# Gated experts with residual: gate loads first, coefficients on GpSimd, operands around the openings made in another way and at other steps

## The chip, the cores and the metric

The kernel runs on one core of a Trainium2 chip. Five engines work side by side, each through its own instructions in order: TensorE (PE in the profile, with its weight loads as PEld), VectorE (DVE), ScalarE (ACT), GpSimd (POOL) and SyncE (SP), which here only issues DMA transfers. ACT issues two transfers as well. The metric is the device time of one execution in microseconds, as the median of several runs. The profile is of one further execution.

## The reference, cut to what matters

For each of 8 batch items `x[b]` (512 rows of 256) there are 8 experts and one shared expert, all of the same form, a gated product with an inner width of 1024:

```python
g = jnp.einsum('bsd,edf->ebsf', h, Wg)
u = jnp.einsum('bsd,edf->ebsf', h, Wu)
expert_outs = jnp.einsum('ebsf,efd->ebsd', jax.nn.silu(g) * u, Wd)
expert_output = jnp.einsum('be,ebsd->bsd', gating_probs, expert_outs)
shared = jnp.einsum('bsf,fd->bsd', jax.nn.silu(h @ Sg) * (h @ Su), Sd)
sg = shared_gate_prob[:, :, None]
return (1.0 - sg) * expert_output + sg * shared     # x + this is the output
```

So each hidden block of expert `e` and item `b` is scaled by one number, `gates[b, e] * (1 - shared_gate[b])`, or `shared_gate[b]` for the shared expert. All data is float32.

## The kernel before, in words

**Units.** The 8 items are worked in two halves of 4. A half runs over 9 experts, an expert over 2 groups of 4 blocks of 128 inner columns. That makes 36 units; a unit is 4 weight blocks against 4 items, for gate (`m = 0`) and up (`m = 1`), followed by the down products. Unit 0 opens the first half and unit 18 the second (`u.opens`); units 17 and 35 close them (`u.closes`).

**Fewer products.** The 256 input columns are two halves of 128, so a plain product of block i and item j takes two matrix products. The kernel takes fewer: it forms weights `at[i] = CI[i] * a + A` with `CI = (0, 1, -1, 2)` from the two halves `a`, `A` of a weight block, and item operands in the same manner (`turn_x`), computes the diagonal i = j (steps P and Q), and for the six pairs of `PAIRS` a shared product (R1) of differences `U`, `V` and two further products (R) of sums `W`, `VB`. This needs sums of operands on POOL and ACT, and of partial results (`z`, `Q`) on DVE and POOL. The down products use sums `T` and `sd` in the same spirit, two parts of four items each, and accumulate over the units of a half in `acc`.

**Item operands.** At the start of a half, `turn_x` transposes each item on PE into PSUM banks `po0`, `po1`, which ACT (line 155) and DVE (157, 159) copy out. The differences `V` and sums `VB` of the items are the same for all units of a half: they are made once, stored to DRAM (`scratch`), and loaded again by later units (lines 201 and 220). In the second half, three of the six pairs are made ahead by `make_forms`, during unit 17, and stored by `store_made`: DVE subtracts (175), ACT scales if needed (177), DVE adds (178), POOL adds (179), SP stores (186).

**Order.** A string of letters sets the order in each unit: a `G` is one step of gate and up, a `D` one down product of the unit before. `nG` counts the G steps, 52 in a unit: 16 for the diagonal and 6 for each pair. PE and POOL follow the program's order throughout (`manual_schedule`), ACT does in unit 0 only. DVE, SP and, after unit 0, ACT are ordered by a planner, by priority in program order and by when it thinks an instruction can run; on the chip each queue is then strictly in that order.

**Weights.** `load_w` brings gate and up of one block (two transfers of 128 KB, lines 261 to 268). `make_at(u, i)` forms the scaled weight: for `CI = 1` and `-1` one POOL operation, for `CI = 2` in all units but unit 0 an ACT scaling (line 280) and a POOL add (281); in unit 0 two POOL adds (290, 291). Blocks 0 to 2 are prepared in the unit before, block 3 at the unit's start (line 562).

**Coefficients.** `make_coef` loads the gates, spread to all partitions, through ACT's queue (lines 102, 107), and DVE makes the 9 x 8 table `coef` (109 to 112). `finish` reads it for each hidden block on DVE (line 361). It is called after the first products (644).

**The start.** `touch_banks` warms PE and ACT, then items and the weights of unit 0 are loaded in turn (lines 634 to 636), item 0 is turned, the P products of block 0 run, and the weights are formed:

```python
    for m in range(2):
        P_step(units[0], 0, m)
    for i in range(NI):
        make_at(units[0], i)
    make_coef()
```

Of the kernel before, what the change touches and what calls it, by code (L numbers as in the profile page):

```python
# [9 lines left out]
F32 = mybir.dt.float32  # L10
AF = mybir.ActivationFunctionType
ALU = mybir.AluOpType
# [4 lines left out]
def kernel(  # L17
# [32 lines left out]
    B, S, D = x.shape  # L50
    E, _, F = Wg.shape
    P = 128
# [5 lines left out]
    CI = (0.0, 1.0, -1.0, 2.0)  # L58
# [7 lines left out]
    const = ctx.enter_context(tc.tile_pool(name="const", bufs=1))  # L66
# [24 lines left out]
    gp = nc.gpsimd  # L91
    ve = nc.vector
# [3 lines left out]

    coef = const.tile([P, NE, B], F32, name="coef")

    def make_coef():

        gt = const.tile([P, B, E], F32, name="gt")
        nc.scalar.dma_start(
            gt.rearrange("p b e -> p (b e)"),
            gates.rearrange("b e -> (b e)").partition_broadcast(P),
        )
        sgt = const.tile([P, B], F32, name="sgt")
        nc.scalar.dma_start(sgt, shared_gate.partition_broadcast(P))
        rest = const.tile([P, B], F32, name="rest")
        ve.tensor_scalar(rest, sgt, -1.0, 1.0, ALU.mult, ALU.add)
        for e in range(E):  # L110
            ve.tensor_mul(coef[:, e, :], gt[:, :, e], rest)
        ve.tensor_copy(coef[:, E, :], sgt)

    scratch = {}
    back = {}
# [52 lines left out]
    def make_forms(h, p):  # L168

        i, j = PAIRS[p]  # L170
        d = CI[i] - CI[j]
        v, b0, b1 = (
            zpool.tile([P, S], F32, tag="z", name=f"f{k}{h}_{p}") for k in range(3)
        )
        ve.tensor_sub(v, xhub[h, i][:, 0], xhub[h, j][:, 0])
        if d != 1.0:
            nc.scalar.mul(v, v, 1.0 / d)
        ve.tensor_add(b0, v, xhub[h, j][:, 1])
        gp.tensor_tensor(b1, v, xhub[h, i][:, 1], ALU.add)
        made.append((h, p, (v, b0, b1)))  # L180
# [48 lines left out]
    def touch_banks():  # L229

        banks = [
            pool.tile([P, S], F32, tag=tag, name=f"touch{tag}{k}")
            for pool, tag, n in ((ps_g, "g0", 3), (ps_g, "g1", 3), (ps_o, "po0", 1), (ps_o, "po1", 1))
            for k in range(n)
        ]
        zero = zpool.tile([P, 2 * S], mybir.dt.bfloat16, tag="z", name="zero")[:, :S]
        ve.memset(zero, 0.0)
        warm = const.tile([P, 1], F32, name="warm")
        nc.scalar.activation(warm, ident[:, 0:1], AF.Silu)
        for bank in banks:  # L240
            nc.tensor.matmul(bank, zero[:, 0:P], zero, start=True, stop=True)
# [4 lines left out]
    units = []  # L246
    for h in range(NH):
        for e in range(NE):
            for g in range(GRP):
                u = Unit()  # L250
# [20 lines left out]
    def scaled_sum(out_, s, a, b, sub):  # L271

        if s in (1.0, -1.0):
            if s == 1.0:
                gp.tensor_tensor(out_, a, b, ALU.subtract if sub else ALU.add)
            else:
                assert not sub
                gp.tensor_tensor(out_, b, a, ALU.subtract)
        else:
            nc.scalar.mul(out_, a, s)  # L280
            gp.tensor_tensor(out_, out_, b, ALU.subtract if sub else ALU.add)  # L281

    def make_at(u, i):
        raw = u.raw[i]
        if CI[i] == 0.0:
            u.at[i] = raw[:, :, 1]
            return
        t = atpool.tile([P, 2, P], F32, tag="at", name=f"at{u.name}_{i}")
        if u.n == 0 and CI[i] == 2.0:
            gp.tensor_tensor(t, raw[:, :, 0], raw[:, :, 1], ALU.add)  # L290
            gp.tensor_tensor(t, t, raw[:, :, 0], ALU.add)
            u.at[i] = t
            return
        scaled_sum(t, CI[i], raw[:, :, 0], raw[:, :, 1], False)
        u.at[i] = t
# [4 lines left out]
    def plain(u, p):  # L300
        return u.n == 0 and p in PLAIN
# [28 lines left out]
    def load_d(u, pairs):  # L330
        for I in pairs:
            t = dpool.tile([P, 2, D], F32, tag="wd", name=f"wd{u.name}_{I}")
            r0 = (NI * u.g + 2 * I) * P
            nc.sync.dma_start(
                t,
                weights(u.e)[2][r0 : r0 + 2 * P].rearrange("(c p) d -> p c d", p=P),
            )
            s = dpool.tile([P, 4, P], F32, tag="sd", name=f"sd{u.name}_{I}")
            a11, a21 = t[:, 0, 0:P], t[:, 0, P : 2 * P]
            a12, a22 = t[:, 1, 0:P], t[:, 1, P : 2 * P]  # L340
            gp.tensor_tensor(s[:, 0], a21, a22, ALU.add)
            gp.tensor_tensor(s[:, 1], s[:, 0], a11, ALU.subtract)
            gp.tensor_tensor(s[:, 2], a11, a21, ALU.subtract)
            gp.tensor_tensor(s[:, 3], a12, s[:, 1], ALU.subtract)
            u.wd[I] = {
                1: a11, 2: a12, 3: s[:, 3], 4: a22, 5: s[:, 0], 6: s[:, 1], 7: s[:, 2]
            }

    def new_bank(u, m, name):
        return ps_g.tile([P, S], F32, tag=f"g{m}", name=f"{name}{m}_{u.name}")  # L350
# [16 lines left out]
    def P_step(u, i, m):  # L367
        bank = new_bank(u, m, f"c{i}{i}")
        u.bank[i, i, m] = bank
        nc.tensor.matmul(  # L370
            bank, u.raw[i][:, m, 0], xhub[u.h, i][:, 0], start=True, stop=True
        )
        t = ppool.tile([P, S], F32, tag="p", name=f"P{i}{m}_{u.name}")
        nc.scalar.copy(t, bank)  # L374
        u.Ps[i, m] = t
        for p in range(ZBANK):
            a, b = PAIRS[p]
            if max(a, b) == i and not plain(u, p):
                new_z(u, p, m, i, bank if u.n or p else None)

    def new_z(u, p, m, i, bank=None):

        o = sum(PAIRS[p]) - i
        z = zpool.tile([P, S], F32, tag="z", name=f"z{i}{o}{m}_{u.name}")
        if bank is None:
            gp.tensor_tensor(z, u.Ps[i, m], u.Qs[o, m], ALU.add)  # L386
        else:
            ve.tensor_add(z, bank, u.Qs[o, m])
        u.z[i, o, m] = z
# [159 lines left out]
    def gate_up(u, nxt):  # L549
# [11 lines left out]
        if u.n:  # L561
            make_at(u, 3)
# [23 lines left out]
        for p in range(len(PAIRS)):  # L586
# [3 lines left out]
            if nxt is not None:  # L590
                if p >= 2:
                    load_w(nxt, p - 2)
                    if p < 5:
                        make_at(nxt, p - 2)
# [34 lines left out]
    by_hand.enter_context(  # L629
        tc.manual_schedule(engines=HAND | {mybir.EngineType.Activation})  # L630
    )
    touch_banks()
    loaded = []
    for i in range(NI):
# [4 lines left out]
        next(turning)  # L639
    for m in range(2):  # L640
        P_step(units[0], 0, m)
    for i in range(NI):
        make_at(units[0], i)
    make_coef()
    behind, acc = iter(()), {}
    for u in units:
        final = u.closes
        nxt = units[u.n + 1] if u.n + 1 < len(units) else None
        g = gate_up(u, nxt)
        nG = 0  # L650
        for what in ORDER if u.n else FIRST:
            if what == "G":
                if nG == 4 and u.n:
                    for _ in behind:
                        pass
                    pv = units[u.n - 1]
                    load_d(pv, (1,))
                    if pv.opens:
                        acc = {}
                    behind = down(pv, acc, pv.closes)  # L660
                    if pv.closes:
                        load_back(pv.h, *BACK[0])
                        since_close = 0
                if final and nxt is not None:
                    if nG == 18:
                        turning = turn_x(u.h + 1, iopool, "io")
                    if nG >= 18 and nG % 3 == 0:
                        next(turning, None)
                    if nG in (42, 45, 48):
                        make_forms(u.h + 1, nG // 3 - 14)  # L670
                    if nG in (45, 48, 51):
                        store_made()
                next(g)
                nG += 1
                if nxt is None and nG in (18, 24, 30, 36, 42):
                    next(behind, None)
            elif u.n == 0:
                for _ in range(2):
                    next(turning, None)
            else:  # L680
                since_close += 1
                if ends and since_close >= BACK_AT[0]:
                    BACK_AT.pop(0)
                    turn_back(*ends.pop(0))
                next(behind, None)
        for _ in g:
            pass
        if u.n == 0:
            by_hand.close()
            by_hand.enter_context(tc.manual_schedule(engines=HAND))  # L690
        for _ in turning:
            pass
# [52 lines left out]
```

## Time and profile before

| what | value |
|---|---|
| median of 3 runs | 2525.23 us (2524.54 to 2525.8) |
| profiled execution, device time | 2527.06 us |
| its span, first to last instruction | 2525.2 us |
| mean granted TensorE clock | 0.998 |
| DMA | 242.94 MB, mean 96 GB/s |
| DVE `h` L361, 576 instructions | 741 ns each |
| POOL add of 128x512 (`z` L386) | 1281 ns each |
| POOL add of 128x256 (`wb` L281) | 741 ns each |
| ACT scaling of 128x256 (`at` L280), 35 instructions | 409 ns each |
| DVE coefficient products (L111), 8 instructions of 128x8 | 158 ns each |

An engine's busy time is the sum of its instructions; its share is of the span. "Idle before" an instruction is put down to the event that ended it. A line such as L361 is a line of the kernel. The chain of waits goes back from the last instruction, at each step to what released it. The busy share is an average over stretches with different limits, so what matters here is where PE, which is busy in nearly all of the span, is not fed.

### The profile page before, as it was taken

How to read it: one execution, taken by the hardware profiler on the slowest of the kernel's cores; microseconds unless marked ns; L12 is line 12 of the kernel's file. 1: busy time of each engine (PE TensorE's matmuls, PEld its weight loads, DVE VectorE, ACT ScalarE, POOL GpSimd, SP SyncE). 2: the span in 40 equal slices, each digit the busy share in tenths (PEclk: the TensorE clock that was granted, in tenths of full speed). 3: DMA queues.
4: the chain of work that ended last, by engine and by line, in shares of the span. 5: the costliest groups of instructions: out<-in, count | busy, mean ns of one | idle time of the engine just before them, and what ended most of it. 6: DMA issues, size and time to landing. Idle time of an engine off the chain costs nothing.

```text
span 2525.2 us, 22097 instructions
## 1 busy us (share of the span) xinstructions
PE 2501.5 (99%) x5900; PEld 1108.5 (44%) x5900; DVE 1491.3 (59%) x2252; ACT 1143.7 (45%) x2081; POOL 1917.4 (76%) x2067
## 2 busy tenths in 40 slices
PE   8999999999999999999999999999999999999999
PEld 3444444444444444444444444444444444444444
DVE  6655555555555555555775555565565555555556
ACT  3344444444444444444333444444444444444443
POOL 5878777777777778777797777777777777777874
PEclk9999999999999999999999999999999999999999
DMA  3422322333333223332434322232233332332322
GB/s 130 135 82 88 96 88 88 96 97 99 96 88 100 88 83 92 88 92 90 156 126 125 92 86 89 87 95 90 84 100 96 100 95 89 99 89 80 88 87 79
DMA packets 181179, 242.94 MB, mean 96 GB/s; under 512 B 13888, under 2 KB 122432, under 8 KB 181056
## 3 DMA queue, kind: packets, MB, share of 16 engines
q1 hardware_dynamic: 180768, 241.49, 31.7%
q8 instruction: 49, 0.80, 0.1%
q14 instruction: 74, 0.61, 0.1%
q10 hardware_dynamic: 288, 0.04, 0.0%
HBM read 227.84 MB, written 13.63 MB: 96 GB/s over the span
## 4 chain that ended last, share of the span: by engine, by line
PE 96%; DVE 2%; DMA 1%; POOL 1%; issue 1%; ACT 0%; SPq 0%; ACTq 0%; DVEq 0%; POOLq 0%
PE po L488 33%; PE c L442 28%; PE c L429 14%; PE c L401 10%; PE c L370 10%; DVE h L361 0%; DMA sgt<-ondB_sharedgateprob_dram 0%; DMA w<-in_L_cond_Wu_dram 0%; DVE c L434 0%; POOL T L461 0%; POOL z L386 0%; DMA xin<-in_x_dram 0%; PE pto L133 0%; DVE c L433 0%; PE c L414 0%
## 5 line engine op out<-in xcount | busy, mean ns | idle before, releaser
L442 PE MATMUL c<-b,wb 128*128 128x512 f32 x1720 | 810.6, 592 | 1.0 <-DVE c L433 0.5
L386 POOL TENSOR_TENSOR z<-P,Q 128x512 f32<-128x512 f32 x430 | 538.8, 1281 | 114.9 <-DVE Q L407 72.5
L361 DVE SCALAR_TENSOR_TENSOR h<-sg,coef,c 128x512 f32<-128x512 f32 x576 | 426.2, 741 | 230.6 <-PE c L442 220.1
L503 ACT COPY acc<-po 128x512 f32<-128x512 f32 x477 | 279.0, 585 | 585.0 <-PE po L488 582.2
L355 ACT ACTIVATE sg<-c 128x512 f32<-128x512 f32 x576 | 342.1, 595 | 372.3 <-PE c L442 196.8
L442 PEld LDWEIGHTS c<-b,wb 128*128 128x128 f32 x1720 | 325.9, 190 | 409.6 <-issue 386.1
L461 POOL TENSOR_TENSOR T<-h,h 128x512 f32<-128x512 f32 x284 | 358.0, 1278 | 135.0 <-PE po L488 91.7
L488 PE MATMUL po<-T,sd 128*128 128x512 f32 x864 | 435.4, 593 | 4.8 <-ACT po L479 3.2
L429 PE MATMUL c<-v,u 128*128 128x512 f32 x860 | 433.7, 592 | 3.0 <-DVE h L361 2.0
L433 DVE TENSOR_TENSOR c<-z,c 128x512 f32<-128x512 f32 x286 | 198.6, 694 | 330.9 <-ACT sg L355 253.5
L461 POOL TENSOR_TENSOR T<-h,T 128x512 f32<-128x512 f32 x284 | 356.1, 1276 | 6.7 <-PE po L488 6.7
L447 DVE TENSOR_TENSOR c<-c,Q 128x512 f32<-128x512 f32 x288 | 200.0, 696 | 187.5 <-PE c L442 187.3
L281 POOL TENSOR_TENSOR wb<-wb,u 128x256 f32<-128x256 f32 x216 | 154.9, 741 | 204.7 <-ACT wb L280 204.7
L488 PE MATMUL po<-h,wd 128*128 128x512 f32 x576 | 293.5, 592 | 0.0
L479 ACT COPY po<-acc 128x512 f32<-128x512 f32 x465 | 274.4, 590 | 39.2 <-DVE acc L505 19.3
L370 PE MATMUL c<-x,w 128*128 128x512 f32 x576 | 279.7, 599 | 1.5 <-ACT sg L355 1.0
L407 DVE TENSOR_TENSOR Q<-c,P 128x512 f32<-128x512 f32 x288 | 197.5, 686 | 106.0 <-ACT sg L355 105.8
L488 PEld LDWEIGHTS po<-T,sd 128*128 128x128 f32 x864 | 163.2, 190 | 210.0 <-issue 186.5
L429 PEld LDWEIGHTS c<-v,u 128*128 128x128 f32 x860 | 163.2, 190 | 209.7 <-issue 187.0
L374 ACT COPY P<-c 128x512 f32<-128x512 f32 x288 | 168.1, 584 | 131.8 <-PE c L370 131.8
L401 PE MATMUL c<-x,at 128*128 128x512 f32 x432 | 202.8, 592 | 0.0
L434 DVE TENSOR_TENSOR c<-c,z 128x512 f32<-128x512 f32 x286 | 198.0, 692 | 0.0
(73 smaller groups left out, 1878.8 us busy)
## 6 DMA issues: line engine op xcount, KB each, us to landing
b<-xs SPq DMA_DIRECT2D x207, 512.0 KB, 3.5
v<-xs SPq DMA_DIRECT2D x207, 256.0 KB, 2.6
w<-in_L_cond_Wg_dram SPq DMA_DIRECT2D x128, 128.0 KB, 3.3
w<-in_L_cond_Wu_dram SPq DMA_DIRECT2D x128, 128.0 KB, 3.3
wd<-in_L_cond_Wd_dram SPq DMA_DIRECT2D x64, 256.0 KB, 2.7
xin<-in_x_dram SPq DMA_DIRECT2D x16, 256.0 KB, 4.2
xs<-b SPq DMA_DIRECT2D x8, 512.0 KB, 3.1
xr<-in_x_dram SPq DMA_DIRECT2D x16, 256.0 KB, 3.1
```

The costliest lines, as they stand in the source:

```text
L355: nc.scalar.activation(s, bank, AF.Silu)
L361: ve.scalar_tensor_tensor(t, u.sg[i, j], coef[:, u.e, b : b + 1], bank, ALU.mult, ALU.mult)
L370: nc.tensor.matmul(bank, u.raw[i][:, m, 0], xhub[u.h, i][:, 0], start=True, stop=True)
L386: gp.tensor_tensor(z, u.Ps[i, m], u.Qs[o, m], ALU.add)
L401: nc.tensor.matmul(bank, u.at[i][:, m], xhub[u.h, i][:, 1], start=False, stop=True, skip_group_check=True,)
L429: nc.tensor.matmul(bank, u.U[p][:, m], u.V[p], start=True, stop=True)
L442: nc.tensor.matmul(bank, u.W[p][:, r, m], u.VB[p][:, r], start=False, stop=True, skip_group_check=True,)
L447: ve.tensor_add(bank, bank, u.Qs[j, m])
L461: eng.tensor_tensor(t, a, b, ALU.subtract)
L479: nc.scalar.copy(po, acc[J, x])
L488: nc.tensor.matmul(po, u.wd[I][x], b, start=first, stop=True, skip_group_check=not first,)
L503: nc.scalar.copy(acc[J, x], po)
```

## The change

It has three parts.

1. The two gate loads leave `make_coef` and become `load_gates`, issued before `touch_banks`. `make_coef` runs on POOL instead of DVE (ten operations) and is called before `make_at` of unit 0, so it comes ahead of it in POOL's order.
2. `make_at` for `CI = 2` uses the two POOL adds in unit 0, in unit 18 (which opens the second half), and in the unit after each, 1 and 19. ACT's scaling (line 280) goes in units 1, 18 and 19.
3. In unit 17 `make_forms` is called at G steps 33, 39 and 45 instead of 42, 45 and 48, and `store_made` at 39, 45 and 51 instead of 45, 48 and 51. The transposes of the next half's items stay at every third step from 18 to 39.

```diff
-    def make_coef():
-
-        gt = const.tile([P, B, E], F32, name="gt")
+    gt = const.tile([P, B, E], F32, name="gt")
+    sgt = const.tile([P, B], F32, name="sgt")
+
+    def load_gates():
         nc.scalar.dma_start(
             gt.rearrange("p b e -> p (b e)"),
             gates.rearrange("b e -> (b e)").partition_broadcast(P),
         )
-        sgt = const.tile([P, B], F32, name="sgt")
         nc.scalar.dma_start(sgt, shared_gate.partition_broadcast(P))
+
+    def make_coef():
+
         rest = const.tile([P, B], F32, name="rest")
-        ve.tensor_scalar(rest, sgt, -1.0, 1.0, ALU.mult, ALU.add)
+        gp.tensor_scalar(rest, sgt, -1.0, 1.0, ALU.mult, ALU.add)
         for e in range(E):
-            ve.tensor_mul(coef[:, e, :], gt[:, :, e], rest)
-        ve.tensor_copy(coef[:, E, :], sgt)
+            gp.tensor_tensor(coef[:, e, :], gt[:, :, e], rest, ALU.mult)
+        gp.tensor_copy(coef[:, E, :], sgt)
...
-        if u.n == 0 and CI[i] == 2.0:
+        if CI[i] == 2.0 and (u.opens or units[u.n - 1].opens):
             gp.tensor_tensor(t, raw[:, :, 0], raw[:, :, 1], ALU.add)
             gp.tensor_tensor(t, t, raw[:, :, 0], ALU.add)
...
+    load_gates()
     touch_banks()
...
     for m in range(2):
         P_step(units[0], 0, m)
+    make_coef()
     for i in range(NI):
         make_at(units[0], i)
-    make_coef()
...
-                    if nG in (42, 45, 48):
-                        make_forms(u.h + 1, nG // 3 - 14)
-                    if nG in (45, 48, 51):
+                    if nG in (33, 39, 45):
+                        make_forms(u.h + 1, (nG - 33) // 6)
+                    if nG in (39, 45, 51):
                         store_made()
```

## The prediction

> **What bounds the kernel now.** I read the page's totals first, then its chain of waits, then the chain and the timeline of the two stretches in which TensorE (PE) is not steadily fed, and last the busy time by stretch.
>
> ```profile
> PE 2501.5 (99%) x5900; PEld 1108.5 (44%) x5900; DVE 1491.3 (59%) x2252; ACT 1143.7 (45%) x2081; POOL 1917.4 (76%) x2067
> PE 96%; DVE 2%; DMA 1%; POOL 1%; issue 1%; ACT 0%; SPq 0%; ACTq 0%; DVEq 0%; POOLq 0%
> ```
>
> PE is the bound: a 128x512 product is two matmul instructions, and in the steady units the weight loads follow each other every 0.429 us. 36 units of 160 matmuls make 5760 x 0.429 = 2471 us; 128 transposes at about 0.15 us add 19. That leaves 2525 - 2490 = 35 us in which PE waits or runs slowly, and only these can change, since the diff touches no matmul. I added up every gap between weight loads beyond 0.429 us: all of it lies before 66 us, between 1190 and 1365 us (the seam between the two halves of the batch), and in the last 30 us. Units 2 to 16 and 20 to 34 have no gap.
>
> The start, in the chain that ended last (start us, us, what):
>
> ```profile
> 8.69 3.93 DMA w<-in_L_cond_Wg_dram
> 12.62 0.02 issue
> 12.64 6.05 DMA sgt<-ondB_sharedgateprob_dram
> 18.69 0.02 issue
> 18.71 0.04 DVE rest L109
> ...
> 20.88 0.60 DVE x L159
> 21.48 0.04 issue
> 21.53 0.73 PE ptx L133 x4
> 22.26 3.35 PE c L370 x4
> 25.60 3.43 PE c L401 x8
> ```
>
> The gate load itself is held until a weight load lands at 12.62, lands after 6.05 us, and VectorE (DVE) sits before its coefficient work; x L159 behind it frees the bank for the last transposes. The same stretch by windows (PE, PEld, DVE, ACT, POOL busy with counts, granted clock, DMA share, GB/s):
>
> ```profile
> 10.00:13.65 3.65, 0.90 (x3) 0.07 (x1) 0.02 (x1) 0.64 (x2) 2.31 (x4) 1.00 1.02 300
> 13.65:18.00 4.35, 4.28 (x13) 2.02 (x14) 1.27 (x2) 1.62 (x3) 3.31 (x5) 0.67 0.81 260
> 18.00:21.50 3.50, 0.88 (x5) 0.64 (x3) 2.76 (x13) 1.17 (x2) 0.00 (x0) 0.92 0.11 41
> 21.50:26.00 4.50, 4.47 (x10) 2.20 (x11) 3.68 (x5) 0.95 (x2) 1.27 (x1) 0.62 0.37 149
> ```
>
> Two holes of about 3 us, and after each a stretch at a clock of 0.67 and 0.62, in which matmuls come every 0.85 us.
>
> The seam, in the same chain and in the list of waits (engine, line, waited for: us in total, times, longest):
>
> ```profile
> 1236.28 1.28 POOL f L179
> ...
> 1237.95 2.63 DMA w<-in_L_cond_Wu_dram
> ...
> 1241.01 0.57 ACT acc L503
> 1241.59 0.02 issue
> 1241.61 0.60 ACT po L479
> 1242.21 0.14 issue
> 1242.35 1.10 PE po L488 x2
> ACT at L280 <- DMA w<-in_L_cond_Wu_dram: 24.0, 11, 7.8
> ```
>
> SP's queue holds the fourth Wu of unit 18 behind a store (L186) of a form that POOL has not made; ACT stands 7.7 us in front of its scaling (L280) for that weight; the copies behind it on ACT are late; PE loses 2.8 us. ACT stands 7.8 us again for unit 19's weight, until 1308.54, and PE loses about 2.0 us between 1307 and 1316.
>
> **The change, part by part.**
>
> *Gate loads first.* The two issues (0.38 and 0.33 us, rows L102 and L107) go ahead of everything on ACT. Its first data work is at 5.82, after 3.59 us of idle time, which hides them and the shifted table load (1.28). In the start loads are held for the landing of the eighth load before them: the twelfth issue on SP is at 7.02 and the fourth load lands at 2.12 + 4.9; the gates, on ACT, are held in the same way at 11.51 and 12.64. Put first, they take two places, so SP's seventh and eighth issue (3.62 and 4.09) will wait for them; loads further on keep their partners. How soon do the gates land? Row, under load: 6.05 us, so 6.8 and 7.2, and SP is held 3.2 us. Row, the first xin into empty queues: 2.6 us, so 3.4 and 3.8, and nothing is held. [...]I take the first xin's row, the nearest in time and load, and keep 3.2 us of hold for the range; the gates' own traffic (1.1% of 16 engines over 20 us) is 0.2 us.
>
> *What the start becomes.* ACT no longer stands from 8.79 to 13.01: the copy of x1 runs at 8.8 to 9.4 and x L159 to 10.1. PE ends its first Q products at 10.74 as now; xin2 has landed (5.08 + 5.2 = 10.3). So: x2's transposes 1.2 us to 11.9, four P matmuls 1.7 to 13.7. Then the last rows: xin3 is issued at 9.27 and 9.74 and lands at 13.5 and 14.05; **that load is late next**, some 0.4 us after PE is ready. Transposes from 14.1 to 15.3, P products to 17.1. With 0.2 us of gate traffic, the Q products that start now at 25.44 start at 17.2: **8.2 us gained**. What follows up to 66 us moves along: its waits (about 7 us, POOL 100% and DVE 100% busy there) hang on PE's own products and stay. If SP is held 3.2 us, xin3 lands at about 16 and the gain is 6.4.
>
> [...] Here holes of 2.8 and 3.1 us sufficed for 0.67 and 0.62; the slow matmuls (eight at 0.85 for 0.43) cost 3.4 of the 8.2 us. [...]
>
> *Coefficients on POOL.* Ten operations on 8 columns. Rows: POOL 0.457 us for 128 and 0.725 for 256 columns, so about 0.21 by that line; bounds 0.10 (its memset of one column) and 0.457. The sum is 2.1 us (1.0 to 4.6). [...] Either is hidden: POOL idles until a weight lands at 9.21; from a landing at 3.8, 4.6 us end at 8.4. Behind them stand make_at and the operands of unit 0, done at 17.04 now and first needed after 17. Even landed at 7.2 and at the upper bound they end at 11.8, which costs PE nothing while at1, then at 12.5, is needed at 17. DVE loses its 3.8 us of wait there and 0.8 us of work.
>
> *Scaling by sums in units 1, 18 and 19.* ACT loses three operations of 0.41 us and their waits; POOL gets an add of 0.73 for each, in place. In unit 18 POOL then waits 2.46 us for a load anyway, in unit 19 3.68; in unit 1 0.47, so 0.26 us of delay, with no PE work on its heels. Without the wait on ACT, the 2.8 us go; the next arrival, sd on POOL at 1242.17, comes earlier, since POOL loses two forms before it. Of the 2.0 us at unit 19 I take 1.5, as DVE is crowded there (9.83 of 10 us busy).
>
> *Forms at steps 33, 39, 45 instead of 42, 45, 48.* POOL's three adds (1.75, 1.25, 1.25) now start at 1231.7, 1236.3 and 1237.5, in a full stretch (10.00 of 10 us busy from 1230). By the transposes of the same steps (1215.3 and 1224.1) the first two go to where POOL is busy 4.28 and 3.75 of 10 us, the third to about 1232. Their nine stores go with them, so do SP's waits for these adds (11.0 us in three), and SP's weights behind them come about 4 us sooner. No PE wait hangs on it once ACT's is gone: 0. [...]
>
> ```profile
> 1209.04 3.70 DVE L175 TENSOR_TENSOR f<-x,x 128x512 f32<-128x512 f32 x1
> 1209.70 2.48 POOL L461 TENSOR_TENSOR T<-h,T 128x512 f32<-128x512 f32 x2
> ```
>
> That add takes 0.7 us elsewhere. [...] I take 0.5 us against, bounds -0.5 and 2.
>
> Sum: 8.2 + 2.8 + 1.5 - 0.5 = **12.0 us**. The span of 2525.2 becomes 2513.2, the profiled run's 2527.06 becomes 2515.1; against the median of 2525.23, **2513.2**.
>
> **Rivals.**
> - *The start alone pays.* The seam's PE loss stays, because POOL (full from 1230) or DVE is as late as ACT was. For: sd L342 ends at 1242.17, only 0.04 us before ACT's copy. Against: POOL has two forms less before it. 2525.2 - 8.2 = 2517.
> [...]
> - *The crowded stretch from 44 to 66 us dissolves too*, if SP and DVE are ordered anew: up to 3 us more, 2510.
> - *Slower.* SP works in one fixed order, and its head waits 1202 us in total for PE at v loads (L201). If the moved stores and loads redraw that order so that in the units without gaps one operand comes late, each of the 30 pays. From 0.4 us each (12 us) the gain is used up; at 0.65, near the smaller single losses of the seam (0.4 and 0.8 us), it is 2525.2 - 12.0 + 19.5 = 2532.7. For: this queue is filled by due times, not by hand. Against: none of the 30 middle units shows a gap, and they have the same loads.
>
> **How the numbers follow.** Forecast 0.60, start alone 0.16, held loads 0.10, more at the crowd 0.08, slower 0.06. A measurement tells 0.2%, 5 us, from no change. Faster by more: 0.91; within: 0.03 (parts of the second and third rival with more lost); slower: 0.06. Held loads and start alone end at 2518.5 with their spread; the bonus at 2509. Range 2509 to 2518.5.
>
> **What would show it.** Right: no DVE wait for sgt; Q products at 17 to 18 us and a clock near 1.00 from 10 to 26; no ACT wait for Wu at 1240 and 1308; sg and acc copies there on time. Wrong: SP idle at 3.6 to 7, another wait before L488 at 1239, or weight loads more than 0.43 us apart in the middle units.

## The result, and the profile after

The changed kernel takes **2516.07 us** (median of 7 runs, 2515.54 to 2520.22); the kernel before took 2525.3 us beside it (7 runs, 2524.54 to 2528.83). The ratio is 0.9964, with a 95% interval of 0.9953 to 0.9976: faster by 9.2 us, 0.36%, where 12.0 were forecast. The profiled execution has a span of 2514.9 us, 10.3 less than before, and a device time of 2517.02. It is set against the profile of before here, as the forecast's sum was; each of the two profiled executions is 1 to 2 us above the median of its kernel.

The page's totals and the chain of waits, by engine:

```profile
PE 2498.6 (99%) x5900; PEld 1108.3 (44%) x5900; DVE 1492.6 (59%) x2242; ACT 1143.4 (45%) x2078; POOL 1922.3 (76%) x2080
PE 97%; DVE 1%; issue 0%; DMA 0%; POOL 0%; ACT 0%; SPq 0%; DVEq 0%; ACTq 0%
```

The number of PE instructions is the same; DVE has ten fewer and ACT three fewer, POOL has thirteen more. PE's share of the chain rises from 96 to 97%. Where the 10.3 us come from is seen when the start of the same weight load is looked up in both timelines of PE, from the first to the last (line numbers after are three to four higher):

| weight load of | before, us | after, us | gained so far |
|---|---|---|---|
| item 0's first transposes | 4.42 | 5.06 | -0.64 |
| P products of block 0 | 6.13 | 7.87 | -1.74 |
| item 1's transposes | 7.75 | 10.02 | -2.27 |
| the Q products that the forecast follows | 25.44 | 18.23 | +7.21 |
| the P products after them | 28.45 | 22.43 | +6.02 |
| a product before the seam's last item | 1215.69 | 1208.93 | +6.76 |
| second half of that item's transposes | 1220.42 | 1215.40 | +5.02 |
| unit 18, behind the wait for `sd` | 1242.85 | 1234.98 | +7.87 |
| unit 19 | 1316.47 | 1306.48 | +9.99 |

The start gave 6.0 us, the seam (the stretch between the two halves of the batch) 4.0. Between 22 and 1200 us nothing moves by more than 0.1 for good. The start in the chain that ended last (start, length, what):

```profile
1.18 5.17 DMA xin<-in_x_dram
...
6.40 1.54 PE ptx L136 x6
7.94 2.67 PE c L373 x4
...
18.37 1.19 DVE v L200
19.56 0.60 DVE z L391
20.16 1.08 DVE v L200
21.24 0.61 DVE z L391
```

The 25 us are no longer held by the gates and DVE's coefficient work, but by the second part of **item 0's own rows**, which now takes 5.17 us to land (2.8 before), and at the end by two differences `v` that stand ahead of the sums `z` on DVE and are slow in this profile. By windows, with the columns as in the forecast:

```profile
10.00:13.65 3.65, 3.65 (x20) 2.34 (x19) 1.33 (x3) 2.04 (x4) 1.51 (x3) 1.00 1.06 315
13.65:18.00 4.35, 4.35 (x20) 2.61 (x19) 4.28 (x7) 2.68 (x5) 4.19 (x6) 1.00 1.03 350
18.00:21.50 3.50, 3.20 (x7) 0.87 (x5) 3.46 (x5) 1.39 (x4) 2.69 (x3) 1.00 0.17 65
21.50:26.00 4.50, 4.10 (x10) 1.95 (x11) 4.13 (x8) 2.24 (x4) 1.58 (x2) 1.00 0.28 117
```

Both holes and both stretches at 0.67 and 0.62 are gone. What the windows from 10 us on don't show is that PE was slow before:

```profile
6.40 1.54 PE L136 MATMUL ptx<-ident,xin 128*128 128x128 f32 x6 [0.64 <-DMA xin<-in_x_dram]
7.87 2.74 PE L373 MATMUL c<-x,w 128*128 128x512 f32 x4
```

Six transposes took 1.54 us and the four P products 2.74, where the same instructions take 0.88 and 1.98 in a second profile of the same program (stores_late, below). The trace's own record of a full clock begins at 9.43 us here, at 4.91 there. POOL's timeline shows the coefficients (in brackets the idle time before, and what ended it):

```profile
6.72 0.20 POOL L112 TENSOR_SCALAR rest<-sgt 128x8 f32<-128x8 f32 x1 [5.41 <-DMA sgt<-ondB_sharedgateprob_dram]
7.00 1.31 POOL L114 TENSOR_TENSOR coef<-gt,rest 128x8 f32<-128x8 f32 x8
8.24 0.19 POOL L115 COPY coef<-sgt 128x8 f32<-128x8 f32 x1
9.57 0.72 POOL L278 TENSOR_TENSOR at<-w 128x256 f32<-128x256 f32 x1 [1.14 <-DMA w<-in_L_cond_Wu_dram]
```

They end at 8.43, and POOL still waits 1.14 us for a weight: hidden, as forecast.

At the seam, ACT's two waits of 7.8 us for `Wu` are gone, and PE's losses behind them with them. A new wait has come. The chain there has one load in it, and SP's timeline shows what stood ahead of it:

```profile
1209.75 5.61 DMA xin<-in_x_dram
```

```profile
1204.32 4.36 SPq L189 DMA_DIRECT2D xs<-f  x3
1208.78 0.37 SPq L204 DMA_DIRECT2D v<-xs  x1
1209.26 0.87 SPq L142 DMA_DIRECT2D xin<-in_x_dram  x2
```

Before, the same rows are issued here:

```profile
1215.78 0.81 SPq L139 DMA_DIRECT2D xin<-in_x_dram  x2
```

Three stores of the first early form, then a `v` load, then the last item's rows. The second part of these lands at 1215.36, and PE waits 1.7 us for it. The queue alone does not make them so late: measured from the product before the last item (1215.69 and 1208.93 in the table) the rows are issued after 0.33 us instead of 0.09. The rest is the landing of the second part, 5.61 us instead of 4.17.

### The profile page after: what moved, and what is told of

Same layout as the page of the kernel before. It is cut to its first block, busy times and chain, and to the rows that moved or that the text cites. A ratio compares the mean times of both kernels' runs of the same rounds, so it can differ in the third digit from the quotient of the medians.

```text
span 2514.9 us, 22103 instructions
## 1 busy us (share of the span) xinstructions
PE 2498.6 (99%) x5900; PEld 1108.3 (44%) x5900; DVE 1492.6 (59%) x2242; ACT 1143.4 (45%) x2078; POOL 1922.3 (76%) x2080
## 4 chain that ended last, share of the span: by engine, by line
PE 97%; DVE 1%; issue 0%; DMA 0%; POOL 0%; ACT 0%; SPq 0%; DVEq 0%; ACTq 0%
PE po L491 34%; PE c L445 29%; PE c L432 14%; PE c L373 10%; PE c L404 10%; DMA xin<-in_x_dram 0%; PE pto L136 0%; PE ptx L136 0%; POOL z L389 0%; DVE h L364 0%; DVE v L200 0%; PE c L417 0%; DVE c L436 0%; DVE c L437 0%; DVE b L216 0%
```

## The experiments

The runs in one table. *Start* is the gain on the profile of before at the P products that began at 28.45 there; *seam* is what is gained between 1200 and 1316 us. Both come from one profile each. The runs were made in four batches, each beside the kernel before, whose median was 2525.91 for the rows that begin with p, 2526.9 from late_gates to coef_dve, 2525.83 from gates_sp to best, and 2525.19 for one_row; so times of different batches are compared by the ratio.

| run | median, us (lowest to highest, runs) | ratio to before, 95% interval | span | start | seam |
|---|---|---|---|---|---|
| the changed kernel | 2516.07 (2515.54 to 2520.22, 7) | 0.9953 to 0.9976 | 2514.9 | 6.0 | 4.0 |
| p1_gates_only | 2521.56 (2520.13 to 2522.81, 10) | 0.9970 to 0.9988 | 2519.1 | 5.9 | -0.2 |
| p2_sums_only | 2520.19 (2517.81 to 2522.89, 10) | 0.9964 to 0.9984 | 2519.5 | -0.4 | 5.9 |
| p3_forms_only | 2523.5 (2520.88 to 2525.62, 10) | 0.9981 to 0.9999 | 2523.7 | -1.8 | 3.0 |
| p12_old_forms | 2514.66 (2513.0 to 2515.86, 4) | 0.9939 to 0.9968 | 2510.9 | 7.9 | 5.9 |
| late_gates | 2516.93 (2515.12 to 2517.32, 4) | 0.9945 to 0.9974 | 2514.8 | 5.9 | 4.2 |
| gates_twice | 2517.53 (2517.32 to 2520.55, 5) | 0.9954 to 0.9980 | 2518.8 | 3.2 | 3.1 |
| z_first | 2516.29 (2514.69 to 2519.44, 4) | 0.9945 to 0.9975 | 2514.0 | 6.5 | 4.4 |
| coef_dve | 2517.28 (2515.2 to 2517.39, 5) | 0.9948 to 0.9976 | 2515.1 | 5.4 | 4.3 |
| gates_sp | 2514.42 (2513.78 to 2515.34, 5) | 0.9945 to 0.9970 | 2512.8 | 6.4 | 5.7 |
| stores_late | 2515.53 (2513.88 to 2517.52, 5) | 0.9951 to 0.9978 | 2511.8 | 7.4 | 5.6 |
| best | 2513.25 (2512.99 to 2514.9, 5) | 0.9942 to 0.9967 | 2511.2 | 7.6 | 5.9 |
| one_row | 2511.99 (2511.88 to 2513.67, 5) | 0.9935 to 0.9962 | 2510.0 | 8.9 | 5.9 |

**The three parts alone.** Each is the kernel before with one part of the diff: the gate loads first with the coefficients on POOL; the sums for `CI = 2`; the forms at the early steps.

> Only the first part of the change on the kernel before: gate loads first, coefficients on POOL. Theory A (the ledger of weight-load times: start +6.0 us, scaling by sums +4.9, early forms -1.0): the products that follow the P products of item 2 start at 18.2 us, the seam is as before, the time is 6.0 us below before, about 2519.3. Theory B (the start's gain is partly lost again to crowding up to 66 us when the rest is as before): 3 to 4 us below before.

> Only the second part: make_at by two POOL adds in units 1, 18 and 19. Theory A: both waits of ACT for Wu vanish by themselves, 4.9 us below before (2.8 near 1239 and 2.1 near 1308), about 2520.4. Theory B (the early forms are needed, because POOL, with two more form adds ahead of sd and T near 1236, is as late as ACT was): 2 to 3 us below before, with PE waiting for POOL near 1239.

> Only the third part: forms at steps 33, 39, 45. Theory A: the load of the last item's rows comes late behind the stores (-1.7 us), the long DVE add beside POOL goes (+0.8), ACT still waits for Wu, which comes about 1 us sooner (+0 to +1): between 1 us slower and equal, 2525 to 2526.5. Theory B (the early stores free SP's queue, as the prediction's step had it): Wu 4 us sooner, ACT's wait nearly gone, 2 to 3 us below before.

Part 1 has its gain at the start and nothing at the seam, where ACT's waits for the weight remain. Its list of waits on ACT, from 1225 to 1320 us (us in total, times, longest):

```profile
ACT at L283 <- DMA w<-in_L_cond_Wu_dram: 16.2, 2, 8.2
```

Part 2 alone takes both away and has 5.9 us at the seam: 2.85 in unit 18, 2.1 in unit 19, and 0.9 before unit 18. The first two are the part's own: all eleven profiles with the sums have them, to within 0.02. The 0.9 is not, in the main. There the first form's `f`, which took 3.70 us in the profile of before, takes 1.25 beside the same `T` of POOL:

```profile
1209.41 1.25 DVE L175 TENSOR_TENSOR f<-x,x 128x512 f32<-128x512 f32 x1
1210.06 3.40 POOL L461 TENSOR_TENSOR T<-h,T 128x512 f32<-128x512 f32 x2
```

Of all 14 profiles only before and gates_twice have the 3.70, whatever their edits. Against before, gates_twice gains nothing up to the last item's rows, p1_gates_only 0.28, and every other run 0.78: this is an accident of the one profile of before, and no gain of a part. Part 2 doesn't need the early forms. Part 3 alone shortens only one of the two waits, that in front of unit 18, from 7.7 us to 2.8; the other is 8.3:

```profile
ACT at L280 <- DMA w<-in_L_cond_Wu_dram: 11.1, 2, 8.3
```

It gains 2.6 us in unit 18, since the weight comes sooner, and loses 0.5 in unit 19; by its times it is 2.4 us faster than before, so of its two theories B fits. The 2.6 is the loss that part 2 removes as well, so the two gains don't add. Its start, whose code is that of before, is 1.8 us later in this profile: a first measure of what one profile can vary by.

**The changed kernel with the forms at the old steps**

```diff
-                    if nG in (33, 39, 45):
-                        make_forms(u.h + 1, (nG - 33) // 6)
-                    if nG in (39, 45, 51):
+                    if nG in (42, 45, 48):
+                        make_forms(u.h + 1, nG // 3 - 14)
+                    if nG in (45, 48, 51):
```

> The changed kernel with the forms and their stores back at the old steps. Theory A: 1.0 us below the changed kernel, about 2515: the transposes of the last item do not wait for their rows (1.7 us), the long DVE add is back (0.8). Theory B (the parts need each other): 2 us or more above the changed kernel.

Without part 3 the seam gives 5.9 us instead of 4.0, and PE doesn't wait for the last item's rows. The times alone don't resolve it (2513.0 to 2515.86 against 2515.54 to 2520.22). The profiles of all runs together do: the four with the sums and the old forms have 5.9, every one, and the seven with the sums and the early forms have 3.1 to 5.7, with a median of 4.3. In five of these seven PE waits 1.3 to 1.8 us for the rows, whose second part then took 5.2 to 5.6 us to land; in the other two it took 3.9 and 4.0.

**Early forms, late stores.** In the changed kernel `store_made` goes back to steps 45, 48 and 51.

> The changed kernel with the forms made at steps 33, 39 and 45, but stored at the old steps 45, 48 and 51. Theory A (the last item's transposes wait 1.7 us at 1215 because the stores of the first forms, waiting for POOL's sum, hold SP in front of that item's loads): the two loads are issued at about 1206 or earlier, the wait for them is below 0.3 us, and the rest of the seam is as in the changed kernel: 1.3 to 1.7 us shorter, span about 2513.3. Theory B (the loads are slow for another reason: the second took 5.6 us to land beside the other traffic): the wait stays above 1 us and the span stays at 2515.

The wait is gone (0.1 us is lost there against before, 1.75 in the changed kernel's profile), but not for the reason of Theory A: in SP's queue the stores stand where they stood, since the planner places them by when it thinks them ready. All five engines have the order of the changed kernel. **This run is a second profile of the changed kernel**, with a span 3.1 us shorter: 1.4 at the start, 1.6 at the rows, which landed in at most 4.0 us instead of 5.6. So the new wait comes and goes from one execution to the next, and the run speaks for neither theory. What makes the rows late when they are late, beyond the 0.25 us of SP's queue, stays open: the transfers that SP issues around them are the same in both profiles.

**Where the gate loads stand.** Four runs. First behind `touch_banks` on ACT:

```diff
-    load_gates()
     touch_banks()
+    load_gates()
```

> The changed kernel with its gate loads issued after the touches, behind ACT's table load, at about 2.2 us instead of 0.73. Theory A (the gates' small packets share the DMA engines with the first item's rows and make these 2.3 us late): the first transposes are back at 4.4 and run through, the P products of item 0 start at 6.2 and not 7.9, and the time is about 1 us below the changed kernel, less than 2.3 because the last item's rows bound the start next. Theory B (what costs is only the hold of SP's queue, whose seventh and eighth load wait for the gates): the gates land later still, the hold moves to later loads, and the time is equal or up to 1 us above the changed kernel.

The first rows come as before the change: transposes at 4.43, P at 6.42. But now ACT's issue of the gates is held for earlier loads, and with it the copy of item 1 behind it. ACT's timeline:

```profile
8.79 0.38 ACTq L103 DMA_DIRECT2D gt<-in_fside_Bx_dram  x1
10.11 0.33 ACTq L107 DMA_DIRECT2D sgt<-ondB_sharedgateprob_dram  x1
10.48 0.58 ACT L158 COPY x<-ptx 128x512 f32<-128x512 f32 x1 [8.25 <-DMA xin<-in_x_dram]
```

What the earlier rows give (2.2 us) ACT's stand takes back, and the start gains 5.9, as good as in the changed kernel: the first transposes are those of Theory A, the time is that of Theory B. Second, both gate loads twice (a second pair of tiles of the same size that nothing reads):

> The changed kernel with both gate loads doubled: a second pair into tiles that nobody reads goes first. Theory A (traffic of small packets): the first item's rows land 2 us later again, the first transposes near 7 and the P products near 10, 1.5 to 2.5 us above the changed kernel. Theory B (the rows were late for another reason, and only the hold counts): the first transposes stay at 5 to 6.4, SP is held two loads earlier, at most 1 us above.

The start falls to 3.2. Item 0 is no later than in the changed kernel (4.90), against Theory A; the loads further on are, and the second P products wait for their weight until 10.28. The profiled execution is the slowest of the five (2520.55, the others 2517.32 to 2518.09), with a granted clock of 0.54 from 10 to 12 us, so 3.2 is at the low end. Third, on SP, behind item 0's rows and the first weight block:

```diff
-        nc.scalar.dma_start(
+        nc.sync.dma_start(
...
-    load_gates()
     touch_banks()
...
         load_w(units[0], i)
+        if i == 0:
+            load_gates()
```

(Both loads of `load_gates` are changed in this way.)

> The changed kernel, with the two gate loads issued by SP behind the first item's rows and the first weight block (fifth and sixth load) instead of by ACT ahead of everything. Theory A (the lost part of the start gain is the place of the loads: ahead of the first rows they delay them by 2.3 us and hold SP's seventh load; far behind they hold ACT): first transposes back at about 4.4 us, first P at 6.2 to 6.5, no stand of ACT between 8.8 and 13, Q products of item 1 at 16.5 to 17.2 (18.23 in the changed kernel), span 1 to 2 us shorter: about 2513.5. Theory B (wherever the gates stand, eight loads may be open and two small ones take two places; the loads behind pay the same): transposes at 4.4, but the later rows (items 1 to 3) late by as much, Q at 18 or later, span 2514.5 to 2516.

Item 0 is early again (4.43, P at 6.39), but item 1's transposes are at 9.85, hardly better than 10.02. The chain has its second row load in it, and the windows show why:

```profile
4.10 6.36 DMA xin<-in_x_dram
```

```profile
4.00:6.00 2.00, 2.00 (x10) 1.38 (x8) 0.35 (x1) 0.00 (x0) 0.00 (x0) 1.00 0.43 78
6.00:8.00 2.00, 1.65 (x5) 0.68 (x4) 0.34 (x1) 1.03 (x2) 0.00 (x0) 1.00 0.50 176
```

While the gates are under way the core's transfers fall to 78 GB/s (198 from 4 to 6 us before the change): Theory B at the start. The lower span comes from the rows of the seam, which landed in time. So the place only chooses *who* is late. What remained was the gates themselves: 288 packets for 36 KB, as the transfers spread both loads to 128 partitions. The list of DMA queues of the changed kernel up to 12 us (packets, MB, share):

```profile
q10 hardware_dynamic: 288, 0.04, 1.8%
```

**The gates in one row, spread by PE.** A last kernel takes that away. It also has the old forms and `z` first, so it is to be compared with the run called best (below), and, for the place of the loads, with p12_old_forms, whose gates also go out on ACT ahead of everything.

```diff
+        nc.scalar.dma_start(
+            row[:, 0:NG], gates.rearrange("b e -> (b e)").partition_broadcast(1)
+        )
+        nc.scalar.dma_start(row[:, NG : NG + B], shared_gate.partition_broadcast(1))
+
+    def spread_gates():
+        gp.memset(ones, 1.0)
+        bank = ps_g.tile([P, S], F32, tag="g1", name="gates")
+        nc.tensor.matmul(bank[:, 0 : NG + B], ones, row, start=True, stop=True)
+        nc.scalar.copy(gall, bank[:, 0 : NG + B])
...
         P_step(units[0], 0, m)
+    spread_gates()
```

> As in best, but the gates come in one row: the two loads (on ACT, ahead of everything, as in the changed kernel) bring 64 and 8 numbers to a single partition, one PE product of a row of ones with that row spreads them to all 128 partitions behind the first P products, and ACT copies the result (128x72) for POOL's coefficient work. Theory A (what the gate loads cost the start is their many small packets, 288 for 36 KB): the dip in the DMA rate between 2 and 7 us goes; first transposes at 4.4 to 4.7 us, first P at 6.1 to 6.5, transposes of item 1 at 7.7 to 8.1 (9.67 in best, 10.02 in the changed kernel, 7.75 before), Q products of item 1 at 16.8 to 17.4 (18.03 in best), where the rows of item 3 take over; span 0.7 to 1.2 us under best's 2511.2: about 2510.2. Theory B (what counts is that two further loads are open, which holds the loads behind them, whatever their size): transposes of item 1 at 9.5 or later, Q at 18 or later, span as in best or above, 2511 to 2512.

Theory A: transposes at 4.44, P at 6.39, the Q products at 16.51 by the weight load (17.86 in best, 17.51 in p12_old_forms). Only item 1's transposes come later than it said, at 8.68 behind the gates' product (best: 9.67, p12_old_forms: 8.99). The queue's packets, the windows, and the chain:

```profile
q10 hardware_dynamic: 4, 0.00, 0.0%
```

```profile
4.00:6.00 2.00, 2.00 (x10) 1.37 (x8) 0.35 (x1) 0.00 (x0) 0.00 (x0) 1.00 0.67 187
6.00:8.00 2.00, 1.65 (x5) 0.68 (x4) 0.34 (x1) 1.03 (x2) 0.00 (x0) 1.00 1.07 346
```

```profile
6.40 1.98 PE c L386 x4
8.38 0.37 PE gates L115 x2
8.75 1.02 PE ptx L145 x8
...
16.68 3.43 PE c L419 x8
20.11 1.72 PE c L386 x4
```

The dip is gone, the two further loads still open among the first eight cost nothing that shows, the spread costs PE 0.37 us, and from 8.4 to 26 us the chain has nothing but PE in it. The edit takes away packets, bytes (36 KB become 288) and the spread to 128 partitions at once; which of them it was, no run separates. This is the fastest version, 13.2 us under before (2525.19 in its runs), and every run of it is under every run of the changed kernel. Its lead on best (12.6) is read from the start alone, 8.9 against 7.6: the two intervals overlap.

**Coefficients on DVE again, at the new place**

```diff
-        gp.tensor_scalar(rest, sgt, -1.0, 1.0, ALU.mult, ALU.add)
+        ve.tensor_scalar(rest, sgt, -1.0, 1.0, ALU.mult, ALU.add)
```

and the same for the products and the copy.

> The changed kernel with the ten coefficient operations back on DVE, in the same place of the program. Theory A (which engine makes them is of no account once the gates come first): DVE makes them from about 6.7 us on in 1.6 us or less; the copy of item 0 at 7.1 may be 1 us later, and the time is within 1 us of the changed kernel. Theory B (the move to POOL is part of the gain): 2 us or more above the changed kernel.

Within 0.2 us of span and 1.2 of median, and the ratios are 0.9962 and 0.9964: the engine makes no difference that shows, the early loads do. (Item 0's copy, behind the coefficients on DVE, makes P begin at 8.19 instead of 7.87.)

**`z` ahead of `v` on DVE.** In unit 0 the differences from the third pair on are ordered behind the last `z`:

```diff
+            if u.n == 0 and p >= 2:
+                with tc.issue_after(last_z[0]):
+                    ve.tensor_sub(v, xhub[u.h, i][:, 0], xhub[u.h, j][:, 0])
```

> The changed kernel with DVE's item differences for pairs 2 and 3 of unit 0 kept behind the two sums z that free the banks of item 2. Theory A (PE loses 1.5 us near 20 us because DVE takes these differences first): PE's two waits there go, 1.2 to 1.5 us below the changed kernel. Theory B (the differences are as urgent as the sums): the loss comes back within unit 0, no difference.

DVE's timeline of this run, with both `z` ahead of the second `v`:

```profile
19.10 1.35 DVE L397 TENSOR_TENSOR z<-c,Q 128x512 f32<-128x512 f32 x2
20.37 1.26 DVE L202 TENSOR_TENSOR v<-x,x 128x512 f32<-128x512 f32 x1
```

PE loses nothing between the Q products and the P products after them, here and in the two later runs that have this edit; in the eight other profiles with early gates it loses 0.0 to 1.2. The order alone is not the loss. In stores_late and p12_old_forms the order is that of the changed kernel and nothing is lost; there the `v` between the two `z` takes 0.68 us instead of 1.16. In stores_late:

```profile
18.52 0.68 DVE L391 TENSOR_TENSOR z<-c,Q 128x512 f32<-128x512 f32 x1
19.12 0.68 DVE L200 TENSOR_TENSOR v<-x,x 128x512 f32<-128x512 f32 x1
19.72 0.68 DVE L391 TENSOR_TENSOR z<-c,Q 128x512 f32<-128x512 f32 x1
```

So the edit takes away a loss that comes in some executions only: the two `v` take 0.67 to 1.73 us each in these profiles, and what that costs hangs on when PE arrives. In the time its gain can't be told, since in this run PE's P products of block 0 were slow. Windows of it, and the same products in PE's timeline, here and then in stores_late:

```profile
8.00:9.00 1.00, 1.00 (x2) 0.34 (x1) 0.00 (x0) 0.00 (x0) 0.49 (x4) 0.50 1.08 306
9.00:10.00 1.00, 1.00 (x2) 0.34 (x1) 0.00 (x0) 0.49 (x1) 0.39 (x1) 0.50 0.97 363
```

```profile
7.65 3.53 PE L377 MATMUL c<-x,w 128*128 128x512 f32 x4 [0.35 <-DVE x L160]
```

```profile
7.67 1.98 PE L373 MATMUL c<-x,w 128*128 128x512 f32 x4 [0.35 <-DVE x L160]
```

The windows laid by the trace's record of the clock (columns as above), first z_first, then stores_late:

```profile
4.53:7.95 3.42, 1.77 (x10) 1.14 (x10) 0.69 (x1) 0.58 (x1) 1.10 (x7) 1.00 0.86 284
7.95:11.36 3.41, 3.41 (x6) 1.29 (x5) 0.00 (x0) 0.73 (x2) 1.26 (x5) 0.50 1.03 321
```

```profile
4.91:8.33 3.42, 1.94 (x10) 1.26 (x11) 0.69 (x1) 0.58 (x1) 1.34 (x9) 1.00 0.88 294
8.33:11.74 3.41, 3.41 (x16) 1.93 (x15) 0.69 (x1) 1.97 (x4) 1.02 (x4) 1.00 1.00 321
```

Both have the same late rows. In z_first a window that held 1.77 us of PE's work was followed by a whole window at half clock, in stores_late one of 1.94 was not; the two windows begin 0.4 us apart.

**Best of the parts**: old forms, gates on SP, `z` first.

> Three things together: the changed kernel with its forms at the old steps, the gate loads on SP as in gates_sp, and the sums z ahead of the differences v on DVE in unit 0. If these gains are separate (1.2 to 1.6 at the last item's transposes, 1 to 2 at the gates' place, 1.5 at z): median 2511 to 2513, 2 to 4 us below the changed kernel's own, interval of the ratio about 0.993 to 0.996. If they run into one another, because the next late load (item 3) takes over at the start: 2513.5 to 2515, as with the forms at the old steps alone (2514.66).

The median of 2513.25 lies between the two expectations, 2.8 us under the changed kernel's and 2.3 under that of stores_late, which is the changed kernel in the same batch. The seam has its full 5.9, `z` costs nothing, and the start is at 7.6, with item 1's late rows in it (9.67).

## Why the prediction was right, and where its sizes were off

- **What bounds the kernel**: right. The 30 middle units have no gap in either kernel, and all that was gained was gained at the start and the seam. The slower case, a new gap in the middle units, did not come.
- **Start, 8.2 us forecast, 6.0 measured (7.4 in the second profile).** Two terms are off. *"The gates' own traffic (1.1% of 16 engines over 20 us) is 0.2 us"*: a share of busy time averaged over the stretch, where the question was what stands beside 288 small packets while they run. They put item 0's rows 2.4 us and item 1's transposes 2.3 us later; 1.0 of this is left at the Q products (7.2 gained there). With the packets taken away the same point gains 8.9. Nor did the gates land like the first rows (2.6 us), as chosen, but in 4.4 and 5.5, nearer the other bound (6.05): SP's seventh load went out at 5.14, when the gates landed, instead of 3.62: the forecast's own sign of being wrong, SP idle at 3.6 to 7, came in part. The case of a held SP, put at a gain of 6.4 at the start, came nearest in size, though its reason, a late item 3, is not what happened. The *missing* term is DVE: with the start shorter, two `v` differences stand ahead of the `z` that PE waits for. This costs 1.2 us in this profile, where both are slow (1.19 and 1.16 us), and nothing in the second, where one of them takes 0.68.
- **"That load is late next" (item 3)**: no. Its transposes came at 15.20, without a wait, since PE was itself late by then.
- **The clock**: the granted clock is 1.00 from 10 to 26 us as forecast. But the forecast, which counts the 3.4 us of the slow matmuls as gained, looked at the two holes of before alone, of 2.8 and 3.1 us. The late rows leave two short waits (1.2 and 1.0 us between weight loads) in front of the P products, and these took 1.98, 2.74, 3.00 or 3.5 to 3.6 us in runs with the same loads ahead of them; in this profile 0.8 us was lost so before 10 us, of which 0.2 is left at the Q products (18.23, and 18.01 in the second profile). The row of the two holes did not foresee this.
- **Coefficients on POOL**: right. They took 1.7 us, 2.1 forecast, and are hidden. One product took 0.205 us, against 0.158 on DVE: 1.3 times. The DVE run shows no worth of the engine either way.
- **Seam, 3.8 forecast, 4.0 measured (5.6 in the second profile)**: right as a sum, by luck, since three errors cancel. The sums were put at 2.8 and 1.5 and give 2.85 and 2.10. Another 0.78 belongs to no part: it is the slow `f` of the profile of before. The early forms were put at 0.5 against, the author's estimate beside an `f` of 3.70 us, and at nothing for SP. No run shows the 0.5: the first `f`, moved with the early forms, takes 1.24 us in the changed kernel beside a `T` of 3.39. What the runs show in its place is a wait for a load. *"No PE wait hangs on it once ACT's is gone: 0"*. One did, the last item's rows, and it cost 1.75 in this profile: 0.25 by their place behind the moved stores in SP's queue, the rest by a slower landing whose cause is not shown. Against the seam of 5.9 with the old forms, the early forms cost 0.2 to 2.8, in the median 1.6 (0.8 of the 2.8, in gates_twice, is the slow `f` again). That is near the bounds given, for another reason; what they bring (2.6 alone, in unit 18) the sums bring anyway.

## What to carry to other kernels

A small load that is spread over all partitions isn't small while loads are what the start waits for: price it by what it does to the loads in flight beside it, not by its bytes or its mean share (here 36 KB in 288 packets put item 1's transposes 2.3 us later, 288 bytes spread by a matrix product of 0.37 us put them 0.9 later). When an edit moves a store in a queue, name every load behind it in that queue, not only those for which there was a wait before. Two parts of a change that remove the same wait have one gain between them, and where one profile differs from the next by 3 us, a part worth 1 or 2 shows only in a point of the timeline that many runs share. A loss that the one profile of before shows may be its own, and not the kernel's: the 0.78 us of the slow `f` would have been booked to a part without the other runs.

## What the runs showed of the hardware that was not expected

- Two loads of 36 KB in 288 packets took 4.4 and 5.5 us to land beside the first rows (the changed kernel), against 6.1 and 6.05 under load before. From 4 to 6 us the core's rate was 78 GB/s where they stood in the stream of the first rows (gates_sp), against 198 before; with 288 bytes in 4 packets it was 187 (one_row).
- The granted clock changed in steps. In the trace's record of the profile of before it is full from 4.92 to 15.16 us, half to 18.57, full to 21.99 and half to 25.40: 10.24 us, then three times 3.41. Of the windows of 3.41 us that this record gives, the two with the holes, in which PE was busy for 1.44 and 0.77 us, were each followed by one at half clock; those with 3.06 and 2.57 were not. In z_first one with 1.77 was, in stores_late one with 1.94 was not: there the same two waits of about 1 us stand ahead of the same four products, which took 3.53 and 1.98 us. What decides between the two was not tested.
- The same rows, issued in the same order behind the same stores, landed in 5.6 us in one execution (the changed kernel) and in 4.0 or less in another (stores_late).
- The same pair of instructions, DVE's subtraction `f` and POOL's two adds `T` that begin 0.65 us later, had two outcomes: 3.70 us for DVE and 2.5 for POOL in two profiles (before and gates_twice), 1.25 and 3.4 in the other twelve.
